# Edge features as they lie in memory, and four small matmuls for the first edge layer in place of one

## The chip, the core and the metric

The kernel runs on one core of a Trainium2 chip. A core has a matrix engine (PE, with its weight loads listed apart as PEld), a vector engine (DVE), an activation engine (ACT), GpSimd (POOL) and a queue engine (SP) that issues transfers. Each runs its own instructions in order and waits for the others by semaphores. The metric is device time in microseconds, and lower is better. Before the change three runs took 4669.65, 4689.0 and 4695.63 us; the median is 4689.0 us.

## The reference

The kernel is one graph layer over 12,500 nodes of 160 features and 400,000 edges, with a residual. What matters here is the path of an edge:

```
h = silu(edge_length_embedded @ fc_W1 / 4)         # 16 features -> 64, for each edge
w = h @ fc_W2 / 8                                  # 64 -> 192 weights, for each edge
mid = products of w, of the source node's row y[src] (160 values) and of four edge attributes
z   = for each node, the sum of mid over the edges that end at it
out = x + C_S * s + C_X * (z @ W_l2)               # s, y: linear maps of relu(layernorm(x))
```

The input `edge_length_embedded` is called `edge_attr_16` in the argument list and `e16` in the kernel. Edges are sorted by their target node. All data is 32-bit floating point.

## The kernel before

**Tiles.** 128 edges make a tile; there are 3125 tiles. Four tiles make a batch (782 batches), and eight batches make a block of features (98 blocks). A window is 24 to 3 consecutive tiles whose target nodes lie close together, and four windows make a group (150 groups). A first stage computes the rows y of all nodes and writes them to memory (some 100 us); then a loop over the batches does the edges.

**A step of the loop.** The order of every engine's instructions is the order in which the program text issues them. Step b does, on the engines named:

- `features(b + 8)`: if that batch opens a new block, SP issues the transfers of the block's features into a tile `xe` (128 partitions x 512). There are two such tiles, so a new block can land only when the block two before it has been read for the last time.
- `weigh(b + 2)`: PE makes the edge weights `pw` of a batch (four matmuls of 64 rows and 192 columns, two in each half of the rows), and ACT copies the edge attributes beside them. There are two `pw` buffers, so PE first waits until DVE has used the batch before the last.
- in the two steps after a group has ended, `linear` (five matmuls into a `px` buffer, copied out by ACT) and `add` (two matmuls).
- `products(b + 1)`: DVE makes the selection matrix `sel` and the products `pr` from `pw` and the gathered rows `yg`.
- `sums(b)`: PE adds the products up by node: one matmul of 128x128 by 320 columns for each tile, into `pz`. When a window is complete, DVE transposes it into `za`.
- `gather`: POOL issues one indirect transfer for each tile, of 128 node rows, four batches ahead. Two of a batch's gathers wait for the second tile's matmul in `sums(b)`, two for the last one.
- in every fourth step (b = 0, 4, 8, ...), `hidden_pair`: the first edge layer for the next four batches. PE runs `hidden(s)` and `hidden(s + 1)`, each for two batches, each into a `px` buffer of its own, and ACT applies silu (`activate`) and so frees the buffer. There are only two `px` buffers, and `linear`, `add` and some smaller steps need them as well.

**The first edge layer.** In memory a block of features is 128 rows of 512 values. The rows are ordered by pair s of batches (4), batch k of the pair (2) and feature (16); the columns are the 512 edges of a batch, in two halves h of 256. The weights `w1` hold `fc_W1` eight times, alternately in columns 0 to 63 and 64 to 127, with zeros elsewhere: in each 32-row group the first 16 rows have weights in the left half, the other 16 in the right half. Before the change the transfers exchange h and k: partition 32s + 16h + feature holds, for both batches, the half h of the edges. One matmul of 32 rows, 128 columns of weights and 512 columns of data then yields both batches, with half h on output partitions 64h to 64h + 63 and batch k in columns 256k to 256k + 255. That is the layout that `weigh` reads.

The change and the prediction touch `features` (L355 to L365), `hidden` (L580), `activate` (L588), `hidden_pair` (L593), `weigh` (L599), `sums` (L626), `linear` (L645) and `gather` (L565).

Of the kernel before, what the change touches and what calls it, by code (L numbers as in the profile page):

```python
# [18 lines left out]
P = 128  # L19
# [3 lines left out]
FC_IN = 16  # L23
FC_H = 64
# [27 lines left out]
def kernel(  # L52
# [19 lines left out]
    nc = tc.nc  # L72
# [63 lines left out]
    w1 = const.tile([P, 2 * FC_H], F32, name="w1")  # L136
# [218 lines left out]
    def features(b):  # L355
        blk = b * GT // BT
        if blk not in blocks:

            xe = ld.tile([P, 512], F32, name="xe")
            v = e16[blk * P:(blk + 1) * P, :].rearrange("(s k f) (h c) -> s h f k c", s=4, k=2, h=2)  # L360
            for s in range(4):
                for h in range(2):
                    lo = 32 * s + FC_IN * h
                    nc.sync.dma_start(xe[lo:lo + FC_IN, :].rearrange("p (k c) -> p k c", k=2), v[s, h])
            blocks[blk] = xe  # L365

    def e4_load(q):
# [28 lines left out]
    with (  # L396
# [88 lines left out]
        for q in range(len(steps) + 7):  # L485
# [9 lines left out]
            if q == 24:  # L495
                for b in range(min(EARLY, NB)):
                    features(b)
# [38 lines left out]
    with (  # L536
# [43 lines left out]
        def hidden(s):  # L580

            xe = blocks[s * 2 * GT // BT]
            r = slice(32 * (s % 4), 32 * (s % 4 + 1))
            ph = p_x.tile([P, 512], F32, name="px")
            nc.tensor.matmul(ph, w1[r, :], xe[r, :], start=True, stop=True)  # L585
            return ph

        def activate(s, ph):  # L588
# [4 lines left out]
        def hidden_pair(s):  # L593

            pair = [i for i in (s, s + 1) if 2 * i < NB]
            for i, ph in [(i, hidden(i)) for i in pair]:
                activate(i, ph)
# [199 lines left out]
        for b in range(NB):  # L797
            g = group_of[b]
            k = b - first_of[g]
            if b + EARLY < NB:  # L800
                features(b + EARLY)
            q, r = divmod(b, KB)
# [4 lines left out]
            u, v = divmod(b, SB)  # L807
# [67 lines left out]
    with (  # L875
# [5 lines left out]
        with tc.For_i(0, n, 1) as _:  # L881
# [8 lines left out]
            with tc.For_i(0, TP // GT, 1) as g:  # L890
                xe = fp.tile([FC_IN, 512], F32, name="f_xe")
# [21 lines left out]
                ph = fpp.tile([FC_H, 512], F32, name="f_ph")  # L913
# [4 lines left out]
                for k in range(GT):  # L918
                    nc.tensor.matmul(pw[:, k, 0:NW], hT[:, P * k:P * (k + 1)], w2[0:FC_H, :],
                                     start=True, stop=True)  # L920
# [37 lines left out]
            with tc.For_i(0, NT, 1) as i:  # L958
# [4 lines left out]
                for c in range(3):  # L963
                    o = 256 + 64 * c
# [62 lines left out]
```

## Time and profile before

| What | us |
| --- | --- |
| median of three runs | 4689.0 |
| profiled execution, whole | 4669.59 |
| its span, first to last instruction | 4667.7 |
| PE busy | 3717.5 (80%) |
| POOL busy | 2963.4 (63%) |
| DVE busy | 2735.8 (59%) |
| ACT busy | 580.9 (12%) |
| hidden's matmuls (L585), busy | 270.3 |

Each matmul of 32-bit data appears in the profile as two passes, each with a weight load of its own, so 391 calls of `hidden` are 782 records. The ends of matmuls are modelled: a pass is listed with its run through the array, and passes that follow each other overlap in the list. The distance between their starts is what a pass occupies. In a row of a group, the first number after the bar is busy time, the second the mean in ns of one, and then comes the idle time before them with what ended it. In a row of the timeline the first number is the start and the second the length, both in us. "Remote" marks a wait whose end the profile could not assign. TensorE was granted 0.885 of its full clock on average.

### The profile page before, as it was taken

Reading aid. Unit: us, or ns where it says so; the run is one execution under the profiler, and the core shown is the slowest. Engines: PE = TensorE matmul, PEld = TensorE weight load, DVE = VectorE, ACT = ScalarE, POOL = GpSimd, SP = SyncE. Lnnn points to the kernel's source line nnn. Section 1 sums busy time; section 2 is a strip of 40 time slices with the busy share of each in tenths; the row PEclk is TensorE's granted clock in tenths of the full one; section 3 lists DMA queues with packets and bytes.
Section 4 is the critical chain, followed back from the end, with each engine's and each line's share of the span. In section 5 each row is a group of like instructions: output and inputs, shape, how many; then the busy total and the mean of one; then the engine's idle time right before and its main releaser. Section 6 shows DMA issues by size and latency. Waiting matters only on the chain.

```text
span 4667.7 us, 53917 instructions
## 1 busy us (share of the span) xinstructions
PE 3717.5 (80%) x17202; PEld 2479.6 (53%) x17202; DVE 2735.8 (59%) x6877; ACT 580.9 (12%) x1845; POOL 2963.4 (63%) x3144
## 2 busy tenths in 40 slices
PE   7787787788877877777887788777877788888877
PEld 7455455455555554554555555555555555555545
DVE  5455555565556555555556566656556666666665
ACT  5111111111111101011101001111011110111100
POOL 5666666666666666666666666666666666666665
PEclk8888988889889888888888888988888898899998
DMA  7222222222222222222222222222222222222223
GB/s 192 69 61 64 64 65 66 65 65 64 62 64 65 69 72 62 67 69 66 68 68 67 65 71 67 68 67 67 65 70 66 68 63 64 68 67 71 63 63 113
DMA packets 262501, 329.03 MB, mean 70 GB/s; under 512 B 82888, under 2 KB 212216, under 8 KB 262216
## 3 DMA queue, kind: packets, MB, share of 16 engines
q0 software_dynamic: 150128, 256.23, 20.6%
q1 hardware_dynamic: 111590, 69.02, 5.2%
q8 instruction: 140, 2.29, 0.2%
q14 instruction: 145, 1.19, 0.1%
q10 hardware_dynamic: 498, 0.30, 0.0%
HBM read 307.67 MB, written 17.61 MB: 70 GB/s over the span
## 4 chain that ended last, share of the span: by engine, by line
PE 60%; another core or an unknown queue 13%; DVE 12%; issue 9%; ACT 2%; POOL 1%; DVEq 1%; ACTq 0%; DMA 0%; SPq 0%; POOLq 0%
PE pz L636 31%; PE pw L606 13%; PE px L649 6%; DVE pr L533 4%; PE px L585 3%; DVE pr L529 2%; PE px L661 2%; DVE za L642 1%; DVE za L643 1%; ACT hT L590 1%; POOL yg L571 1%; DVE own L620 1%; PE px L707 1%; PE px L706 1%
## 5 line engine op out<-in xcount | busy, mean ns | idle before, releaser
L571 POOL DMA_INDIRECT yg<-y_d,src_q x3061 | 2897.7, 947 | 1642.4 <-issue 803.1
L636 PE MATMUL pz<-pr,sel 128*128 128x320 f32 x6250 | 2069.0, 478 | 61.7 <-DVE za L643 39.6
L636 PEld LDWEIGHTS pz<-pr,sel 128*128 128x128 f32 x6250 | 1254.8, 211 | 607.6 <-issue 248.8
L606 PE MATMUL pw<-w,hT 64*128 64x192 f32 x6250 | 782.2, 368 | 508.3 <-DVE pr L533 276.0
L606 PEld LDWEIGHTS pw<-w,hT 64*128 64x128 f32 x6250 | 538.7, 198 | 953.3 <-issue 792.2
L642 DVE STREAM_TRANSPOSE za<-pz 128x160 f32<-128x160 f32 x598 | 205.5, 344 | 1034.8 <-PE pz L636 438.5
L533 DVE TENSOR_TENSOR pr<-pw,yg 128x384 f32<-128x384 f32 x1532 | 774.0, 547 | 0.0
L529 DVE TENSOR_TENSOR pr<-pw,yg 128x512 f32<-128x512 f32 x766 | 524.1, 684 | 192.5 <-DMA yg<-y_d,src_q 177.8
L622 DVE TENSOR_TENSOR sel<-own,pw 128x512 f32<-128x512 f32 x782 | 537.0, 687 | 27.0
L524 ACT ACTIVATE pw<-ev 128x20 f32<-128x20 f32 x782 | 149.5, 191 | 2957.7 <-PE pw L606 972.2
L649 PE MATMUL px<-wo,za 128*128 128x160 f32 x1500 | 330.7, 384 | 178.5 <-ACT hT L590 149.6
L649 PEld LDWEIGHTS px<-wo,za 128*128 128x128 f32 x1500 | 284.6, 247 | 220.1 <-ACT hT L590 165.0
L620 DVE TENSOR_TENSOR own<-iota,pw 128x128 f32<-128x128 f32 x782 | 199.6, 255 | 247.6 <-ACT pw L524 209.4
L585 PE MATMUL px<-xe,w 32*128 32x512 f32 x782 | 270.3, 658 | 63.0 <-ACT os L651 33.6
L590 ACT ACTIVATE hT<-px 128x512 f32<-128x512 f32 x391 | 220.2, 594 | 554.9 <-PE px L585 173.9
L643 DVE STREAM_TRANSPOSE za<-pz 32x160 f32<-32x160 f32 x598 | 202.2, 338 | 20.5
L672 DVE SCALAR_TENSOR_TENSOR acc<-px,a_sb,acc 128x160 f32 x300 | 114.1, 380 | 120.0 <-remote 33.6
L585 PEld LDWEIGHTS px<-xe,w 32*128 32x128 f32 x782 | 72.4, 189 | 177.7 <-issue 99.1
L661 PE MATMUL px<-os,place 128*128 128x160 f32 x600 | 133.3, 349 | 35.8 <-ACT os L651 24.2
L661 PEld LDWEIGHTS px<-os,place 128*128 128x128 f32 x600 | 94.1, 205 | 76.1 <-issue 41.7
L715 DVE SCALAR_TENSOR_TENSOR acc<-px,look,acc 128x160 f32<-128x160 f32 x98 | 33.1, 379 | 131.2 <-PE pz L636 38.3
L651 ACT ACTIVATE os<-px 128x160 f32<-128x160 f32 x150 | 44.9, 300 | 349.5 <-PE pz L636 91.2
(128 smaller groups left out, 1435.0 us busy)
## 6 DMA issues: line engine op xcount, KB each, us to landing
yg<-y_d,src_q POOLq DMA_INDIRECT x3061
xe<-in_e SPq DMA_DIRECT2D x784, 32.0 KB
xs<-in_x SPq DMA_DIRECT2D x48, 160.0 KB
acc<-in_x SPq DMA_DIRECT2D x11, 640.0 KB
y_d<-ys SPq DMA_DIRECT2D x11, 640.0 KB
out<-acc SPq DMA_DIRECT2D x11, 640.0 KB
raw<-in_e SPq DMA_DIRECT2D x32, 192.0 KB
src_q<-in_src SPq DMA_DIRECT2D x32, 48.0 KB
```

The source lines that it names most:

```text
L529: nc.vector.tensor_mul(pr[:, :n, :].rearrange("p t (x u) -> p t x u", x=2)[:, :, :, 0:M0], wt[:, :n, 0:NW].rearrange("p t (x u) -> p t x u ...
L533: nc.vector.tensor_mul(pr[:, :n, D * x + M0:D * (x + 1)].rearrange("p t (c u) -> p t c u", c=3), wt[:, :n, 96 * x + M0:96 * (x + 1)].unsqu ...
L571: fetch = nc.gpsimd.indirect_dma_start(out=yg[:, slot(t), :], out_offset=None, in_=y_d, in_offset=bass.IndirectOffsetOnAxis(ap=ev4[t // BL ...
L585: nc.tensor.matmul(ph, w1[r, :], xe[r, :], start=True, stop=True)
L590: nc.scalar.activation(hT, ph, AF.Silu, scale=1.0 / math.sqrt(FC_IN))
L606: nc.tensor.matmul(pw[:, k, 0:NW], hT[r, o:o + P], w2[r, :], start=True, stop=True)
L622: nc.vector.tensor_tensor(sel, own[:, :n, :].unsqueeze(2).to_broadcast([P, n, 4, WN]), wt[:, :n, NW:NW + 4].unsqueeze(3).to_broadcast([P, ...
L636: mm = nc.tensor.matmul(pz[:, 0:PC], sel[:, slot(t), :, :], pr[:, slot(t), :], start=o == 0, stop=last)
L642: nc.vector.transpose(zT[g][:, :, at_w], pz[:, D:PC].rearrange("p (k u) -> p k u", k=ZK))
L643: nc.vector.transpose(zT[g][0:32, :, at_w], pz[0:32, 0:D].rearrange("p (k u) -> p k u", k=ZK))
L649: nc.tensor.matmul(po[:m, :], za[:, k, :m], wo[:, k, :], start=k == 0, stop=k == ZK - 1)
L661: nc.tensor.matmul(ps[:, h, :], place[:m, h, :], os[:m, :], start=True, stop=True)
```

## The change

A block of features now comes in one transfer, row for row as it lies in memory, in place of eight that exchange h and k. So partition 32s + 16k + feature holds batch k with all its 512 edges. `hidden` does the exchange: for each k and h a matmul of its own takes the 32 rows of the group, the 64 columns of weights that are nonzero for batch k, and the 256 columns of half h, and writes output partitions 64h to 64h + 63, columns 256k to 256k + 255. The result in `px` is the same as before, and nothing behind it changes.

```diff
-            v = e16[blk * P:(blk + 1) * P, :].rearrange("(s k f) (h c) -> s h f k c", s=4, k=2, h=2)
-            for s in range(4):
-                for h in range(2):
-                    lo = 32 * s + FC_IN * h
-                    nc.sync.dma_start(xe[lo:lo + FC_IN, :].rearrange("p (k c) -> p k c", k=2), v[s, h])
+            nc.sync.dma_start(xe, e16[blk * P:(blk + 1) * P, :])
...
-            nc.tensor.matmul(ph, w1[r, :], xe[r, :], start=True, stop=True)
+            for k in range(2):
+                for h in range(2):
+                    o = slice(FC_H * h, FC_H * (h + 1))
+                    nc.tensor.matmul(ph[o, 256 * k:256 * (k + 1)], w1[r, FC_H * k:FC_H * (k + 1)],
+                                     xe[r, 256 * h:256 * (h + 1)], start=True, stop=True)
```

On PE, this is a stretch around one hidden pair of the program before (L585 is `hidden`, L606 `weigh`, L649 `linear`, L771 and L772 a smaller map, L636 `sums`; the last column is the shape of the output):

```order
L636 MATMUL pz<-pr,sel 128x320 x4
L585 MATMUL px<-xe,w_93 128x512 [waits DMAHW2_49,DMAHW1_49]
L585 MATMUL px<-xe,w_93 128x512 [waits DMAHW4_49,DMAHW3_49]
L606 MATMUL pw<-w_94,hT 128x192 [waits DVE_49,Activation_49]
L606 MATMUL pw<-w_94,hT 128x192 x3
L649 MATMUL px<-wo,za 128x160 [waits Activation_49]
L649 MATMUL px<-wo,za 128x160 x4
```

The same stretch of the changed program, where `hidden` is L584:

```order
L636 MATMUL pz<-pr,sel 128x320 x4
L584 MATMUL px<-xe,w_93 64x256 x8
L606 MATMUL pw<-w_94,hT 128x192 [waits DVE_49,Activation_49]
L606 MATMUL pw<-w_94,hT 128x192 x3
L649 MATMUL px<-wo,za 128x160 [waits Activation_49]
L649 MATMUL px<-wo,za 128x160 x4
```

Eight matmuls stand where two stood, four for `hidden(s)` and behind them four for `hidden(s + 1)`; the neighbours keep their order.

On SP, a stretch of transfers in the middle of the program before (L364 loads `xe`, L372 to L376 the attributes and indices of 96 tiles, L390 stores an index table):

```order
L364 DMA xe<-in_e 16x2x256 x8
L372 DMA raw<-in_e 128x384
L374 DMA src_q<-in_src 128x96
L376 DMA dst_q<-in_dst 128x96
L364 DMA xe<-in_e 16x2x256 x16
L390 DMA drel_d<-drel 128x96
```

The same stretch of the changed program:

```order
L360 DMA xe<-in_e 128x512
L368 DMA raw<-in_e 128x384
L370 DMA src_q<-in_src 128x96
L372 DMA dst_q<-in_dst 128x96
L360 DMA xe<-in_e 128x512 x2
L386 DMA drel_d<-drel 128x96
```

Each run of eight has become one transfer; nothing changes places. The orders on ACT, DVE and POOL stay as they were.

## The prediction

> **What bounds the kernel now.** I read the page's busy shares first, then the groups, the chain, the waits of the lines that the change touches, and last the timeline of single steps.
>
> ```profile
> PE 3717.5 (80%) x17202; PEld 2479.6 (53%) x17202; DVE 2735.8 (59%) x6877; ACT 580.9 (12%) x1845; POOL 2963.4 (63%) x3144
> PE 60%; another core or an unknown queue 13%; DVE 12%; issue 9%; ACT 2%; POOL 1%; DVEq 1%; ACTq 0%; DMA 0%; SPq 0%; POOLq 0%
> L571 POOL DMA_INDIRECT yg<-y_d,src_q x3061 | 2897.7, 947 | 1642.4 <-issue 803.1
> L585 PE MATMUL px<-xe,w 32*128 32x512 f32 x782 | 270.3, 658 | 63.0 <-ACT os L651 33.6
> ```
>
> PE leads in busy time and on the chain, and hidden has 270.3 us of it. But POOL is close behind: gathers follow each other 1.25 us apart (0.95 us and a gap of 0.30; 3014.81 and 3016.06 in the last fence of this part), and 3061 x 1.25 = 3826 us is 82% of the span, though the page counts 63% as busy. So PE and POOL hold each other up, and what a microsecond on PE costs depends on the step. Here is a step with a hidden pair:
>
> ```profile
> 3011.77 0.43 PE L636 MATMUL pz<-pr,sel 128*128 128x320 f32 x1
> 3012.13 1.13 PE L585 MATMUL px<-xe,w 32*128 32x512 f32 x4
> 3013.19 0.92 PE L606 MATMUL pw<-w,hT 64*128 64x192 f32 x8
> ```
>
> The pair occupies PE from 3012.13 to 3013.19, 1.06 us. A query that ends at 3012.14 already shows two of its four passes begun:
>
> ```profile
> 3012.13 0.70 PE L585 MATMUL px<-xe,w 32*128 32x512 f32 x2
> ```
>
> So hidden(s) and hidden(s + 1), which use different 32-row groups, run side by side; each has two passes in a row. Behind the pair things often stand still:
>
> ```profile
> 3033.92 1.13 PE L585 MATMUL px<-xe,w 32*128 32x512 f32 x4
> 3035.36 0.92 PE L606 MATMUL pw<-w,hT 64*128 64x192 f32 x8 [0.31 <-issue]
> 3040.97 1.08 ACT L590 ACTIVATE hT<-px 128x512 f32<-128x512 f32 x2 [2.69 <-remote]
> 3041.61 3.04 PE L649 MATMUL px<-wo,za 128*128 128x160 f32 x10 [5.33 <-ACT hT L590]
> ```
>
> Silu starts nearly 6 us after the pair's last pass (3033.92 + 1.13 = 3035.05), and linear, which needs the px buffer that silu frees, starts behind that. Here 0.9 us more on PE would be seen by nobody. In other steps it would be the last thing waited for:
>
> ```profile
>   PE px L585: 173.9, 83
>   remote: 160.0, 53
>   issue: 98.0, 35
> ...
>   ACT hT L590: 314.6, 92
> ```
>
> The first three rows are what ended the idle time before silu (L590), the fourth what linear (L649) waited for. There are 391 / 2 = 195.5 pairs; 83 idle times were ended by the pair's own matmul.
>
> **The change part by part.** *Matmuls.* First the price of a column. Three and four passes of 320 columns take
>
> ```profile
> 1999.61 0.97 PE L636 MATMUL pz<-pr,sel 128*128 128x320 f32 x3
> 2999.75 1.24 PE L636 MATMUL pz<-pr,sel 128*128 128x320 f32 x4
> ```
>
> so one pass more costs 0.27 us, 0.84 ns a column. A pass of 512 columns is then 0.43 us and the pair's two 0.86; the other 0.20 of the 1.06 us are the start of a new shape, which stays. A pass of 256 columns is 0.215 us. Each hidden now has four matmuls of two passes, eight in its row group. No row shows two matmuls with the same rows and different output columns. The bounds:
> - left and right half run side by side, as the row groups do: four slots of 0.215, 0.86 us, no change;
> - they take turns, row groups still side by side: 8 x 0.215 = 1.72, that is 0.86 us more for each pair, 195.5 x 0.86 = 168 us more on PE;
> - hidden(s + 1) doesn't start before hidden(s) either: 16 x 0.215 = 3.44, 2.58 us more, 504 us in all.
>
> I take the second. It is nearest to the rows: passes overlap there where the rows differ (L585, L606) and follow one another where the rows are the same (L636).
>
> *What of it lies on the path.* The pair is last for silu in 83 of 195.5 cases, 42%, which gives 0.42 x 168 = 71 us as the low end; the high end is all 168, since PE works in order and weigh, linear and sums queue behind the pair, while POOL's gathers wait for sums. I take 90 us, near the low end because the counted row gives that, with a little for pairs that become last by being longer. In the rest, what covers it is the idle time of the rows marked remote and issue above.
>
> *Weight loads.* Four per pair become sixteen, of 64 columns. I cost them at nothing beyond the passes:
>
> ```profile
> 3009.78 1.91 PEld L636 LDWEIGHTS pz<-pr,sel 128*128 128x128 f32 x8 [0.22 <-issue]
> 3009.78 2.42 PE L636 MATMUL pz<-pr,sel 128*128 128x320 f32 x8
> ```
>
> Eight loads on the same 128 rows lie inside the eight passes. The Trainium skill, TensorE: Matmul & The Clock Gate, Part 3, says that a weight load overlaps a running matmul only where the row group differs, which speaks against this change; by that rule these eight would follow one another, 1.91 + 8 x 0.27 = 4.1 us instead of 2.42, so the trace disagrees. By the rule the pair would grow by another 8 x 0.12 = 0.96 us (half of 1.91 / 8 for half the columns), and the sum by as much again as the second bound.
>
> *Transfers.* 784 become 98, of 256 KB each as before in eights. SP needs some 0.4 us to issue one, whatever its shape:
>
> ```profile
> 3019.84 3.76 SPq L364 DMA_DIRECT2D xe<-in_e  x8
> 3023.70 0.39 SPq L682 DMA_DIRECT2D xs<-in_x  x1
> ```
>
> So SP is free 3.76 - 0.39 = 3.4 us earlier in each block, and what is queued behind (attributes, indices, drel) is issued that much sooner. I cost it at nothing. The loop's 94 stretches of four batches that contain such a run, and the 94 between them (first and last row, and the sum, of each):
>
> ```profile
> 217.76:239.23 21.47, 17.63 (x86) 11.69 (x84) 12.67 (x38) 3.63 (x12) 13.25 (x15) 0.92 0.29 79
> ...
> 4539.32:4560.52 21.20, 18.99 (x88) 12.39 (x87) 11.87 (x31) 2.55 (x11) 12.03 (x13) 0.88 0.64 191
> sum 2179.43, PE 1796.03 PEld 1199.53 DVE 1330.95 ACT 269.05 POOL 1394.00; mean PE 19.11 PEld 12.76 DVE 14.16 ACT 2.86 POOL 14.83
> ...
> 239.23:263.39 24.16, 15.54 (x74) 9.85 (x72) 13.74 (x29) 3.15 (x10) 15.31 (x17) 0.94 0.23 61
> ...
> 4560.52:4584.48 23.96, 19.59 (x85) 12.60 (x83) 14.44 (x35) 2.31 (x8) 15.38 (x18) 0.86 0.83 249
> sum 2187.29, PE 1696.33 PEld 1105.81 DVE 1239.69 ACT 230.32 POOL 1396.20; mean PE 18.05 PEld 11.76 DVE 13.19 ACT 2.45 POOL 14.85
> ```
>
> The mean is 23.19 us with the run and 23.27 without; over the neighbouring pairs of stretches the difference is -0.08 with a standard error of 0.37. Removing seven of eight transfers is thus worth 0.08 +/- 0.74 us a block at two errors: at most 0.66 x 98 = 65 us gained, 80 lost, and I take 0. If that cover fails, the first to be late is silu, since a hidden matmul now waits for the whole block and not for two of its eight pieces; but the program issues a block eight batches, some 47 us (2 x 23.2), ahead.
>
> *Sum.* 4669.6 (profiled) + 90 + 0 + 0 = 4760. The median of the runs lies 19.4 us above the profiled one, so 4779.
>
> **The rivals.**
> 1. *The halves run side by side.* For it: PE does so for row groups (two passes at 3012.13). Against: there each pass reads rows of its own; here two read the same rows. Time: 4689, with a start of one slot for the second half 0.215 x 195.5 = 42 us on PE, 0.42 of it on the path, up to 4707. The same page of the Trainium skill, in its table of advice, says that matmuls with few output columns run concurrently in different column groups and gives 2.38 times for three; no run here shows it.
> 2. *Nothing overlaps.* For it: eight instructions now stand between hidden(s) and the end of hidden(s + 1), where the overlap seen skips one. 504 us on PE; half is hidden as in my own case: 4689 + 250 = 4940.
> 3. *Faster: the run of eight transfers holds up the others.* In the fence of SP's rows the eight end at 3023.60, and around that moment three engines resume:
>
> ```profile
> 3023.48 0.19 ACT L524 ACTIVATE pw<-ev 128x20 f32<-128x20 f32 x1 [3.04 <-remote]
> 3023.66 0.35 DVE L642 STREAM_TRANSPOSE za<-pz 128x160 f32<-128x160 f32 x1 [4.67 <-remote]
> 3023.84 0.95 POOL L571 DMA_INDIRECT yg<-y_d,src_q  x1 [3.08 <-remote]
> ```
>
> If the run causes this, a block saves up to 3.08 - 0.30 = 2.78 us. Against it stand the two sums above, which leave at most 0.66 us a block: 4689 - 65 = 4624. It decides from 0.24 us a block (23.4 / 98), if the matmuls cost nothing.
>
> **How the numbers follow.** Half a per cent, 23 us (4666 to 4712), is about what can be told from no change. Halves taking turns: 0.42; its range is 4689 + 40 to 4689 + 168, and 0.04 of it lies under 4712. Side by side: 0.26, of which 0.20 ends within half a per cent and 0.03 on either side. Nothing overlaps: 0.13. Faster by the transfers: 0.13. The remaining 0.06, causes that I don't see, I halve between faster and slower. Faster: 0.13 + 0.03 + 0.03 = 0.19; same: 0.04 + 0.20 = 0.24; slower: 0.57. The range of 4640 to 4860 takes in my own case to its upper bound and the second; it leaves out the 0.13 above and about 0.06 below. The first case alone gives 4729 to 4857.
>
> **What would show it.** In the profile after, a hidden pair occupies 1.9 us from its first pass to weigh (1.06: rival 1; 3.6: rival 2), with the starts of left and right passes 0.215 us apart or together. More silus are ended by the pair's matmul, and POOL waits longer in those steps. Stretches with a load are as long as those without. I am wrong if the pair is 1.9 us and the time the same (then the standstill covers it all), or if gaps like that at 3023 are gone.

## The result, and the profile after

The changed kernel takes 4740.2 us (median of 7 runs, 4715.2 to 4762.8), the kernel before 4678.7 us in the runs shared with it (7 runs, 4668.2 to 4695.6). The ratio is 1.0132, with a 95% interval of 1.0113 to 1.0150: 62 us slower. The forecast of 4779 us (+1.9%) had the direction and the range right. The mechanism that it rested on isn't there, so the number was met by luck. The profiled execution of the changed kernel took 4735.15 us, 65.6 more than the profiled one before, and is the one read here.

The page of the changed kernel, its busy times, its chain that ended last, and the groups that answer to those shown of before:

```profile
PE 3812.4 (81%) x19548; PEld 2575.2 (54%) x19548; DVE 2736.7 (58%) x6877; ACT 599.1 (13%) x1845; POOL 2962.9 (63%) x3144
PE 65%; issue 11%; DVE 11%; another core or an unknown queue 10%; ACT 1%; POOL 1%; DMA 1%; DVEq 1%; ACTq 0%; SPq 0%; POOLq 0%
L567 POOL DMA_INDIRECT yg<-y_d,src_q x3061 | 2897.2, 946 | 1712.2 <-issue 787.6
L584 PE MATMUL px<-xe,w 32*64 32x256 f32 x3128 | 276.4, 397 | 59.5 <-ACT os L651 21.0
```

Hidden's matmuls grew from 782 to 3128 passes, but their busy time went only from 270.3 to 276.4 us, where the forecast wanted some 168 more. POOL does the same work (2897.2 us) and waits 69.8 us longer (1712.2 against 1642.4): about the whole difference of the two spans, 65.7 us. PE's listed busy time grew by 94.9 us, of which `weigh` (L606) has 70.7 and hidden 6.1. The rows of `weigh` in the pages, before and after:

```profile
L606 PE MATMUL pw<-w,hT 64*128 64x192 f32 x6250 | 782.2, 368 | 508.3 <-DVE pr L533 276.0
L606 PE MATMUL pw<-w,hT 64*128 64x192 f32 x6250 | 852.9, 373 | 466.7 <-issue 239.9
```

The granted clock of TensorE, in the view of the cores, is 0.874, against 0.885 before. So the time is lost somewhere, but not in the pair. The timeline of PE around one pair after the change:

```profile
2296.85 1.11 PE L584 MATMUL px<-xe,w 32*64 32x256 f32 x16
2297.89 0.43 PE L606 MATMUL pw<-w,hT 64*128 64x192 f32 x1
2298.55 0.32 PE L606 MATMUL pw<-w,hT 64*128 64x192 f32 x1 [0.23 <-issue]
2299.96 0.41 PE L606 MATMUL pw<-w,hT 64*128 64x192 f32 x1 [1.10 <-issue]
2301.39 0.33 PE L606 MATMUL pw<-w,hT 64*128 64x192 f32 x1 [1.02 <-issue]
2302.79 1.04 PE L606 MATMUL pw<-w,hT 64*128 64x192 f32 x4 [1.07 <-issue]
2303.76 1.43 PE L636 MATMUL pz<-pr,sel 128*128 128x320 f32 x2
```

The pair's sixteen passes occupy PE from 2296.85 to 2297.89, 1.04 us, as long as its four longer passes did before (1.06). Sixteen passes one behind the other would need 3.44 us, and with only the row groups side by side 1.72. So the left and right halves run side by side as well. The starts of the single passes in the trace show it: they come in four groups of four, within 0.04 us in a group and some 0.2 us from group to group. Their weight loads lie inside:

```profile
2296.85 0.65 PEld L584 LDWEIGHTS px<-xe,w 32*64 32x64 f32 x16 [0.44 <-issue]
```

What is new stands behind the pair: `weigh`, whose eight passes start within 0.6 us elsewhere, is drawn out over nearly 6 us, each gap marked "issue", which means that the profile shows nothing that PE waits for. The other engines resume only after that, in the same timeline with all engines:

```profile
2302.90 0.19 ACT L520 ACTIVATE pw<-ev 128x20 f32<-128x20 f32 x1 [11.44 <-remote]
2302.91 0.35 DVE L642 STREAM_TRANSPOSE za<-pz 128x160 f32<-128x160 f32 x1 [2.35 <-remote]
2303.06 1.32 ACT L590 ACTIVATE hT<-px 128x512 f32<-128x512 f32 x2
2303.14 0.95 POOL L567 DMA_INDIRECT yg<-y_d,src_q  x1 [2.68 <-remote]
```

The transpose of `pz` and the gather need work of PE that ended before 2296.9; silu needs the pair, done at 2298. All of them start within 0.25 us of each other, 5 to 6 us after that work of PE, though DVE and POOL had work of their own until 2300.5. Such common late starts are in the kernel before too (3023.5 to 3023.8 in the prediction); the drawn-out `weigh` is not. I counted it in both traces: of the 196 runs of hidden followed by `weigh`, 62 now take over 1.5 us from `weigh`'s first to its last start, and 1 did before; the mean is 1.62 us against 0.74, which is 172 us in sum. The clock doesn't start it: 58 of the 62 begin at the full granted clock. The waits of the lines concerned, before:

```profile
POOL yg L571 <- PE pz L636: 319.1, 184, 6.4
PE pw L606 <- DVE pr L533: 276.0, 139, 6.6
PE pw L606 <- issue: 179.5, 117, 6.2
```

and after (total us, times, longest):

```profile
POOL yg L567 <- PE pz L636: 412.0, 209, 9.0
ACT hT L590 <- remote: 318.2, 72, 15.2
PE pw L606 <- issue: 239.9, 250, 5.9
ACT hT L590 <- PE px L584: 192.1, 75, 6.6
PE pw L606 <- DVE pr L529: 180.0, 128, 5.7
```

`weigh` stands 60 us longer with no releaser shown, in twice as many places, and 96 us less for DVE's products: a part of the new idle time falls into a wait that was there anyway. POOL waits 93 us longer for `sums`. Silu's waits that the pair itself ended are fewer (75, from 83), not more; those marked remote doubled (318.2 us from 160.0). These names are to be read with care, since many of the records from which they are inferred are missing in the two traces (numbers at the end of the part on the prediction).

### The profile page after: what moved, and what is told of

The parts are those of the page before. It is cut to its first block, busy times and chain, and to the rows that moved or that the text cites. A ratio compares the mean times of both kernels' runs of the same rounds, so it can differ in the third digit from the quotient of the medians.

```text
span 4733.4 us, 57379 instructions
## 1 busy us (share of the span) xinstructions
PE 3812.4 (81%) x19548; PEld 2575.2 (54%) x19548; DVE 2736.7 (58%) x6877; ACT 599.1 (13%) x1845; POOL 2962.9 (63%) x3144
## 4 chain that ended last, share of the span: by engine, by line
PE 65%; issue 11%; DVE 11%; another core or an unknown queue 10%; ACT 1%; POOL 1%; DMA 1%; DVEq 1%; ACTq 0%; SPq 0%; POOLq 0%
PE pz L636 32%; PE pw L606 15%; PE px L649 7%; DVE pr L529 4%; PE px L584 3%; DVE pr L525 2%; PE px L661 2%; DVE za L642 1%; DVE za L643 1%; DVE own L620 1%; ACT hT L590 1%; POOL yg L567 1%; PE px L707 1%; PE po L452 1%
## 5 line engine op out<-in xcount | busy, mean ns | idle before, releaser
L567 POOL DMA_INDIRECT yg<-y_d,src_q x3061 | 2897.2, 946 | 1712.2 <-issue 787.6
L636 PE MATMUL pz<-pr,sel 128*128 128x320 f32 x6250 | 2082.0, 480 | 61.1 <-DVE za L643 32.6
L636 PEld LDWEIGHTS pz<-pr,sel 128*128 128x128 f32 x6250 | 1261.2, 212 | 614.7 <-issue 256.4
L606 PE MATMUL pw<-w,hT 64*128 64x192 f32 x6250 | 852.9, 373 | 466.7 <-issue 239.9
L606 PEld LDWEIGHTS pw<-w,hT 64*128 64x128 f32 x6250 | 564.9, 200 | 868.4 <-issue 752.6
L649 PE MATMUL px<-wo,za 128*128 128x160 f32 x1500 | 342.8, 393 | 148.2 <-ACT hT L590 94.7
L649 PEld LDWEIGHTS px<-wo,za 128*128 128x128 f32 x1500 | 295.5, 256 | 199.8 <-ACT hT L590 118.4
L590 ACT ACTIVATE hT<-px 128x512 f32<-128x512 f32 x391 | 231.4, 597 | 809.9 <-remote 318.2
L584 PE MATMUL px<-xe,w 32*64 32x256 f32 x3128 | 276.4, 397 | 59.5 <-ACT os L651 21.0
L584 PEld LDWEIGHTS px<-xe,w 32*64 32x64 f32 x3128 | 131.2, 134 | 196.7 <-issue 114.5
L347 POOL DMA_INDIRECT xr<-in_x,xi x64 | 60.8, 950 | 36.8 <-issue 13.7
```

The costliest lines, as they stand in the source:

```text
L567: fetch = nc.gpsimd.indirect_dma_start(out=yg[:, slot(t), :], out_offset=None, in_=y_d, in_offset=bass.IndirectOffsetOnAxis(ap=ev4[t // BL ...
L584: nc.tensor.matmul(ph[o, 256 * k:256 * (k + 1)], w1[r, FC_H * k:FC_H * (k + 1)], xe[r, 256 * h:256 * (h + 1)], start=True, stop=True)
L590: nc.scalar.activation(hT, ph, AF.Silu, scale=1.0 / math.sqrt(FC_IN))
L606: nc.tensor.matmul(pw[:, k, 0:NW], hT[r, o:o + P], w2[r, :], start=True, stop=True)
L636: mm = nc.tensor.matmul(pz[:, 0:PC], sel[:, slot(t), :, :], pr[:, slot(t), :], start=o == 0, stop=last)
L649: nc.tensor.matmul(po[:m, :], za[:, k, :m], wo[:, k, :], start=k == 0, stop=k == ZK - 1)
```

## The experiments

The theories, with the letters that some expectations use: A, the number of passes and weight loads on PE costs; B, the halves take turns in the array, as forecast; C, the single transfer costs; D, the late hand-overs come from transfers in flight; E, the lateness belongs to the chip, and the kernel only meets it. A hand-over is the moment at which another engine goes on with what PE has finished.

The experiments ran on four chips. On three of them the kernel before takes 3969 to 3973 us, on the fourth 4715 us, so each experiment is compared with the kernel before on its own chip. On which chip the first comparison ran isn't on record; by its time of 4679 us it was none of the three, and it may have been the fourth. It is called the first chip here.

### The transfer alone

```diff
-            v = e16[blk * P:(blk + 1) * P, :].rearrange("(s k f) (h c) -> s h f k c", s=4, k=2, h=2)
-            for s in range(4):
-                for h in range(2):
-                    lo = 32 * s + FC_IN * h
-                    nc.sync.dma_start(xe[lo:lo + FC_IN, :].rearrange("p (k c) -> p k c", k=2), v[s, h])
+            nc.sync.dma_start(xe, e16x[blk * P:(blk + 1) * P, :])
```

The features lie in the exchanged order already, in an input `e16x`; the one matmul stays.

> One transfer for a block, but one matmul for two batches as before: the host hands the features over in the order that the single matmul wants. If the number of passes on PE costs the time (theory A: 16 passes of a pair in place of 4 hold up what PE starts next) or the halves in truth take turns in the array (theory B): as before, 4679 +/- 15. If the single transfer of a block costs it (theory C, a hidden matmul waits for the whole block): as the changed kernel, about 4740.

Measured: 3967.2 us against 3973.1, ratio 0.9988 [0.9978, 0.9997]. The single transfer costs nothing here; it gains some 6 us, little beyond what can be told. What sets the end on this chip is another thing than on the first; the page's chain, and the waits of DVE for gathered rows and of POOL for `sums`:

```profile
DMA 26%; PE 25%; DVE 22%; issue 16%; POOL 10%; DVEq 1%; ACT 0%; POOLq 0%; SPq 0%; ACTq 0%
```

```profile
DVE pr L526 <- DMA yg<-y_d,src_q: 1022.0, 631, 5.1
POOL yg L568 <- PE pz L633: 71.7, 190, 3.7
```

The gathers carry it: DVE waits 1022 us for gathered rows (on the first chip 178 us for the same line, whose idle time is 192.5 us in all), and POOL hardly waits for PE.

### The matmuls alone, and parts of them

Four matmuls for each hidden with the eight transfers kept, so that the output is mixed up but the work on PE is that of the changed kernel:

```diff
-            nc.tensor.matmul(ph, w1[r, :], xe[r, :], start=True, stop=True)
+            for k in range(2):
+                for h in range(2):
+                    o = slice(FC_H * h, FC_H * (h + 1))
+                    nc.tensor.matmul(ph[o, 256 * k:256 * (k + 1)], w1[r, FC_H * k:FC_H * (k + 1)],
+                                     xe[r, 256 * h:256 * (h + 1)], start=True, stop=True)
```

> Eight transfers as before, but four small matmuls for two batches. The output mixes up halves and batches, since both the transfers and the matmuls exchange them; the work is that of the changed kernel's PE. Theories A and B: about 4740, as the changed kernel. Theory C: 4679, as before.

Measured: 3983.3 us, ratio 1.0028 [1.0017, 1.0040]; a repeat on another chip

> Eight transfers and four small matmuls once more, for the case that the chip is one with late hand-overs (the kernel before at 4680 us): there, 1.013 if the matmuls alone cost what the change cost, 1.000 if the single transfer did. On a chip without them: 1.003 again, and nothing new on the late hand-overs.

gave 3978.6 against 3968.8, 1.0031 [1.0019, 1.0044]. The pair occupies 1.03 us, and `weigh` behind it is not drawn out (timeline of PE, first chip of the two):

```profile
2032.91 1.11 PE L588 MATMUL px<-xe,w 32*64 32x256 f32 x16
2033.94 0.92 PE L610 MATMUL pw<-w,hT 64*128 64x192 f32 x8
```

So here the matmuls cost some 10 us, less than half a per cent. B falls by the length of the pair; A's price isn't tested, since no hand-over is late on these chips.

Halves by output column only, with all 512 columns of data:

```diff
+            for h in range(2):
+                o = slice(FC_H * h, FC_H * (h + 1))
+                nc.tensor.matmul(ph[o, :], w1[r, o], xe[r, :], start=True, stop=True)
```

> The kernel before, its one matmul split into two of 64 output columns and all 512 columns of data: 8 passes for a pair, left and right half in the same rows. Theory B: the halves take turns for 0.86 us more a pair, about 4740 as the changed kernel. Theory A: a third of the changed kernel's added passes (4 of 12), about 4700.

Measured: 3975.5 us, 1.0006 [0.9997, 1.0016]. The eight passes of a pair take as long in the list as the four before (1.13 us):

```profile
2030.06 1.09 PE L587 MATMUL px<-xe,w 32*64 32x512 f32 x8
```

They occupy 1.02 us in the median. Two matmuls on the same 32 rows with different output columns run side by side.

The same count of passes without different output columns, four matmuls of 128 data columns each, all 128 output columns:

```diff
+            for c in range(0, 512, 128):
+                nc.tensor.matmul(ph[:, c:c + 128], w1[r, :], xe[r, c:c + 128], start=True, stop=True)
```

> The kernel before, its one matmul split into four of 128 columns with all 128 output columns: 16 passes for a pair as in the changed kernel, no two in the same rows and different output columns, and no more columns in all than before. Theory A (number of passes): about 4740. Theory B (halves take turns): 4679 to 4700, since nothing takes turns that didn't before.

Measured: 3981.8 us, 1.0020 [1.0010, 1.0030]. Here the pair does take longer:

```profile
2056.84 1.71 PE L586 MATMUL px<-xe,w 32*128 32x128 f32 x16
2058.52 0.92 PE L607 MATMUL pw<-w,hT 64*128 64x192 f32 x8
```

1.68 us for sixteen passes, where the data alone would be 8 x 0.107 = 0.86 with the row groups side by side. The starts of the single passes in the trace, as medians over 195 pairs, tell why. On one row group the passes follow each other 0.112 us apart, hardly more than their data. But the second row group starts only beside the fifth of the first group's eight passes, 0.55 us after the first, so the two run side by side for a part of the time only. Doubled again, eight matmuls of 64 data columns:

> The kernel before with its one matmul split into eight of 64 columns: 32 passes for a pair in place of 4, no more columns, no column groups. Theory A (what costs is the number of passes): 28 added passes in place of 12, so 28/12 of the changed kernel's loss, 1.005 on the chip without late hand-overs and 1.03 on one with them. Theory B (halves in the same rows take turns): no loss beyond that of the shorter passes, under 1.003 on either.

Measured: 4090.2 us, 1.0309 [1.0291, 1.0326].

```profile
2084.71 3.66 PE L586 MATMUL px<-xe,w 32*128 32x64 f32 x32
2088.30 1.65 PE L607 MATMUL pw<-w,hT 64*128 64x192 f32 x8
```

This pair occupies 3.59 us; the median is 3.32. Passes on one row group are again 0.112 us apart, with half the data, so something other than the data sets that pace. The load of 128 columns that each pass brings is the likely thing, but no run separates it. The second row group starts beside the thirteenth of the first group's sixteen passes, and in the stretch where both run the passes alternate some 0.055 us apart. Neither expectation (1.005 and under 1.003) foresaw that. So this kernel doesn't test the count as such; it adds some 440 us to PE (2.26 us x 195), of which 121 us show in the time, a little over a quarter. By then PE is the bound: the page's chain has 77% PE.

### The price of PE's time

Every hidden matmul is issued twice, so the pair gets the 0.86 us of the forecast without anything else changing.

> The kernel before with each matmul of hidden done twice into the same place: 8 passes for a pair and 0.86 us more of PE, which is what my prediction took the change to add. On the chip without late hand-overs POOL sets the pace and the pair's step has room: under 1.005 (20 us of 168). With late hand-overs: 1.015 to 1.035, the prediction's 71 to 168 us.

> Each matmul of hidden twice, once more. With late hand-overs: 1.015 to 1.035 (71 to 168 us for 0.86 us of PE a pair, by my prediction); 1.000 to 1.007 if the gaps hide the pair. On a chip without them: 1.002 again.

Measured: 3977.0 us, 1.0017 [1.0008, 1.0027], and on another chip 3974.4 us, 1.0011 [1.0001, 1.0020]. The pair occupies 1.92 us, the number of the prediction:

```profile
2024.75 1.13 PE L585 MATMUL px<-xe,w 32*128 32x512 f32 x4
2025.71 1.03 PE L586 MATMUL px<-xe,w 32*128 32x512 f32 x4
2026.67 0.92 PE L607 MATMUL pw<-w,hT 64*128 64x192 f32 x8
```

168 us more on PE are worth 4 to 7 us on these chips, 3 to 4%, not 42 to 100%. POOL's gathers set the pace there, and PE has room.

### Without the gathers

From the seventh batch on, the changed kernel reuses the rows gathered for the first six.

```diff
+        kept = {}
...
+            if b >= 6:
+                rows[b] = kept[b % 6]
+                return
...
-            yg = rows[b]
+            yg = kept[b] = rows[b]
```

> The changed kernel without the gathers of batches 6 and on, which use the rows of the first six again, so the sums are of wrong rows; everything else is as in the changed kernel. If late hand-overs come with POOL's transfers, none is left, on either chip, and PE alone sets the pace: 782 x 3.2 us for weigh and sums, 195 x 1.04 for the pairs, 150 x 2.4 for linear and add and some 250 for the rest, about 3300 us. If they don't, a chip that has them keeps its gaps and stays above 4000.

Measured: 3316.4 us, 0.8355 [0.8338, 0.8372] of the kernel before. The page's busy times and its chain that ended last:

```profile
PE 3227.2 (97%) x19548; PEld 2223.5 (67%) x19548; DVE 2701.6 (82%) x6877; ACT 570.6 (17%) x1845; POOL 88.6 (3%) x107
PE 82%; DVE 14%; issue 2%; DMA 1%; SPq 0%; POOL 0%; ACT 0%; DVEq 0%; ACTq 0%; POOLq 0%
```

Now PE sets the end. So 650 us lie between PE's bound and the time of these chips, and they are the gathers': that is, as I read it, the cover under which the doubled matmuls vanished.

### The changed kernel on another chip

> The changed kernel itself, beside the kernel before on the same chip. The four runs of the first study were on a chip where the kernel before takes 3973 us and no hand-over from PE was late. On such a chip the parts add up (0.9988 for the single transfer, 1.0028 for the four matmuls): 1.0016, same within half a per cent. On a chip where the kernel before takes 4680 us, with hand-overs up to 13 us late: 1.013 again.

Measured: 3966.9 us against 3969.2, 0.9995 [0.9985, 1.0004]: no difference. The view of the cores, the waits of POOL for `sums`, and PE around a pair:

```profile
core 0: 3966.4 us, clock 0.961
```

```profile
POOL yg L567 <- PE pz L636: 78.2, 195, 4.3
```

```profile
2020.79 1.11 PE L584 MATMUL px<-xe,w 32*64 32x256 f32 x16
2023.01 0.92 PE L606 MATMUL pw<-w,hT 64*128 64x192 f32 x8 [1.11 <-ACT hT L590]
```

`weigh` is drawn out in 1 of 196 cases (62 on the first chip), and the wait in front of it has a name, silu. The same program, then, costs 1.3% on one chip and nothing on another, where the kernel before itself takes 15% less.

### More transfers in flight

In every second batch SP loads a block of features once more, in eight transfers, into a tile that nothing reads: four times as many additional runs as the kernel has of its own. Once with the kernel before, once with the changed one:

```diff
+            if b % 2 == 0:
+                xx = spare_p.tile([P, 512], F32, name="xx")
...
+                        nc.sync.dma_start(xx[lo:lo + FC_IN, :].rearrange("p (k c) -> p k c", k=2), v[s, h])
```

> The kernel before, and in every second batch SP loads a block's features once more, in eight transfers, into a tile that nobody reads: five runs of eight per block in place of one. If PE's hand-overs become late where many transfers are in flight (theory D, which would explain the first chip by transfers alone), late ones appear here on a chip that has none, silus and weigh's copies start microseconds after PE has ended, and the time rises by several per cent. If lateness belongs to the chip or its state (theory E): no late hand-over, 1.000 to 1.01.

> The changed kernel with the same extra transfers. Theory D: the changed kernel is again about 1.013 of the kernel before under the same load. Theory E: the same as the run beside it within 0.003.

These two runs fell on the chip on which the kernel before takes 4715 us. Measured: 4744.1 us, 1.0079 [1.0048, 1.0110], and for the changed kernel 4852.8 us, 1.0293 [1.0262, 1.0325] of the kernel before without the traffic, that is 1.02 of the one with it. The waits of `weigh` and of POOL, first of the kernel before with the traffic:

```profile
POOL yg L572 <- PE pz L637: 396.4, 229, 7.5
PE pw L607 <- issue: 254.8, 141, 5.7
```

then of the changed kernel with it:

```profile
POOL yg L568 <- PE pz L637: 573.7, 257, 9.3
PE pw L607 <- issue: 291.5, 213, 6.2
```

391 additional runs of eight cost 29 us together, 0.07 us each, so the 98 that the change merges are worth some 7 us by this. That speaks against D; a chip without late hand-overs, on which the additional transfers were to tell D from E, didn't come. E expected the two runs within 0.003 of each other, but for a chip without lateness. Beside this traffic the change costs as on the first chip or more, and in the same place: `weigh` drawn out in 36 of 196 cases (1 of 196 with the kernel before), POOL 177 us longer behind `sums`.

## Why the prediction was right or wrong

*The bounds of the pair: wrong choice.* "They take turns, row groups still side by side" is the step that failed. Of the three bounds the first held, the one that I put at 0.26: the pair occupies 1.04 us after the change, 1.03 with the matmuls alone, 1.02 with two column halves, where the second bound needs 1.92. I reasoned that passes overlap where the rows differ and follow one another where they are the same, but the row for the latter (`sums`) has the same rows and the same 128 columns; it said nothing on different columns. The sentence of the Trainium skill that I cited, TensorE: Matmul & The Clock Gate, in its table of advice, that matmuls with few output columns run concurrently in different column groups, agrees with these traces: four passes at once, for 32-bit data and 64 columns.

*Weight loads at nothing: right.* Sixteen of them lie within 0.65 us under the pair. That holds for loads of 64 columns under passes of 256. With loads of 128 columns, passes of 64 columns come no faster than passes of 128 (0.112 us apart), so there the loads may count.

*The share on the path: wrong on two chips, untested where hand-overs are late.* I took 90 of 168 us. Doubling the matmuls added just that 0.86 us for each pair and cost 4 to 7 us in all. The count of silus that the pair ended (83) was no measure of the path, since on those chips the gathers absorb the delay. A doubled matmul never ran on a chip with late hand-overs.

*Transfers at nothing: right as far as measured.* The single transfer alone gives 0.9988 where it could be tried, and additional runs of eight cost 0.07 us each. The two sums over the stretches with and without a load had said 0.08 +/- 0.74.

*The pace of the gathers: read rightly.* The two rows that the prediction takes it from stand in the timeline of the kernel before:

```profile
3014.81 0.95 POOL L571 DMA_INDIRECT yg<-y_d,src_q  x1 [0.30 <-issue]
3016.06 0.94 POOL L571 DMA_INDIRECT yg<-y_d,src_q  x1 [0.30 <-issue]
```

That PE and POOL hold each other up holds for the first chip. On the three others the gathers set the time, and the share on the path had no term for that.

*What would show it.* The signs of the mechanism didn't come: the pair has its old length, and fewer silus are ended by it. POOL does wait longer for `sums`, but not because the pair is longer. Stretches with a load are as long as those without, as foreseen (every other stretch of four batches, 23.39 and 23.74 us, with a standard error of 0.39 on the difference).

*Then why slower?* The total was near the forecast by accident: +62 us measured, +90 forecast, from something no step of mine contained. What is shown: in both comparisons in which PE's results reach the others late, the changed kernel is 1.3% and 2% slower (the latter beside the additional traffic); what has grown is the step with the pair, and new behind the pair is that PE starts `weigh`'s passes some 0.7 to 1.4 us apart with nothing shown that it waits for. From the traces I counted the time from a batch's first `sums` pass to the next batch's, by place in the four batches of a pair's cycle: before 9.12, 4.97, 4.76, 4.36 us, after 9.89, 4.96, 4.56, 4.16. The step with the pair grew by 0.77 us, 150 us over 195 pairs, and 0.41 us of it come back in the other three. That the drawn-out `weigh` is what costs the time isn't shown: in the changed kernel's trace the four batches take 23.56 us on average where it is drawn out (61 cycles) and 23.57 where it isn't (134), with standard errors of 0.25 and 0.24, against 23.22 before. With the traffic they take 25.12 and 24.00, against 23.57 for the kernel before. So the loss comes where these drawn-out passes come, but not cycle by cycle with them. On the chip of 3969 us neither the drawn-out `weigh` nor a loss is there. Rival 1 has the mechanism right, but what it says of the time, no change, holds only for the chips without that lateness.

*What stays open.* What makes PE slow behind the pair, whether that is the whole of the loss, and whether the sixteen passes, the four column tiles at once, or the single transfer sets it off: the parts of the change ran only on chips where none of it costs. That it is the number of instructions (32 matmuls and loads within 1.04 us, in place of 8) is a guess. The traces make two other causes unlikely. One is a lower clock, since 58 of the 62 drawn-out runs begin at full clock. It may still be a part of the loss: TensorE spent 1195 us of the span at half clock in place of 1074, and passes of `sums` are 0.533 us apart there in place of 0.269. The other is the loading of instructions: a packet of the queues that bring them falls into only 8 of the 62, between the pair's first pass and `weigh`'s last. One observation points in a direction. The late traces hold 21,000 to 29,000 records of semaphore updates, those of the others with gathers 65,000 to 75,000; the same kernel left 21,315 on the first chip and 64,812 on the other. Most of what is missing are landings of transfers (14,229 of the changed kernel's are there, and 55,088 on the other chip), but updates by DVE are missing too (2,544 there, in place of 4,198). That something on the way of these updates or of their records is congested is a guess. The Trainium skill, NOTIFIC — the notification-queue block, section 7.1, says that this block's pipeline of event records can hold up the engines that produce them; no run here shows whether it did.

## What to carry to other kernels

Read an overlap from a row in which the thing in question really differs: passes on the same rows follow one another when they use the same columns, and run side by side when their output columns differ, so splitting a matmul into column halves was free on PE (1.04 us for sixteen short passes, 1.06 for four long ones), and splitting its data alone was not (1.68 us for sixteen). Price a microsecond of a busy engine by adding one (on two chips 168 us of PE were worth 4 to 7), not by counting the waits that it ends. A cause that no step of the forecast contains can still give the forecast its number: compare the mechanism, and the same pair of kernels on a second chip, before believing it; here the single transfer with one matmul, 0.9988, is the only version that beat the kernel before, and by little more than can be told.

## What the runs showed of the hardware that was not expected

- The same kernel takes 3969 to 3973 us on three chips and 4679 and 4715 us in two other comparisons, 18 to 19% more, with a granted TensorE clock of 0.97 against 0.88. Whether that belongs to a chip or to the hour isn't shown. In the late traces the records of PE's updates come in bursts of three or more, each within 0.12 us of the one before: 272 in the kernel before, 274 after the change, 298 and 319 with the traffic. The middle half of them begin 1.7 to 2.3 us after the end of POOL's last gather. The traces of the other chips have none.
- Behind the sixteen short passes of a pair, in those late traces only, PE itself starts passes 0.7 to 1.4 us apart, in 62 and 36 of 196 cases. The four long passes of the kernel before leave it at 1 of 196 in such traces too.
- Passes with 128 output columns on the same 32 rows come 0.112 us apart, whether they have 128 or 64 data columns. A second row group's passes start only beside the fourth from last of the first group's, so a pair of 16 such passes takes 1.68 us, one of 32 takes 3.3 to 3.6, where four long ones with the same data take 1.06.
